# A recurrent cell's candidate product with its weights stationary, r and z in one PSUM bank, and z taken late as 1 - z

## The chip, the cores and the metric

The kernel runs on one NeuronCore of a Trainium2 chip. The metric is device time in microseconds (us): the median of several runs of the program. A profile of one execution comes with it; its times count from the first instruction.

The engines are named as in the profile: PE is TensorE's matmul, PEld its weight load, DVE is VectorE, ACT is ScalarE, POOL is GpSimd, SP issues most DMAs. Each engine runs its own instructions in the order in which the program lists them, and waits where an operand is not yet there.

## The reference

Four layers stand one behind the other, each added to its input x of shape 8 x 512 x 256 (batch, time, features), all in float32: a mixture of experts, a gated Haar transform, an adapter with low-rank weights made from a condition, and a gated recurrent unit over the 512 time steps. Only the last one is touched:

```
def step(H, xs):                       # 512 times, H is 8 x 256
    xz, xr, xh = xs                    # X @ Wx.T + bx, for all steps
    Z = sigmoid(xz + H @ Whz.T + bhz)
    R = sigmoid(xr + H @ Whr.T + bhr)
    H_tilda = tanh(xh + R * H @ Whh.T + bhh)   # (R * H) @ Whh.T
    H_new = Z * H + (1.0 - Z) * H_tilda
    Y = H_new @ Whq.T + bhq
    return (H_new, Y)
```

Step s needs the state of step s - 1, so the 512 steps cannot overlap each other.

## The kernel before

The time axis is cut into 16 windows of 32 steps. The first three layers of a window are a few hundred pieces of work ("jobs") on PE, ACT, DVE, POOL and SP. A prologue computes window 0 and the condition's weights. Then one Python loop writes out the 512 recurrent steps (L1362 to L1493), and between the instructions of a step it puts jobs of the later windows and of the output product (`Whq`, L1252). The order on each engine is written by this loop: `jobs.fill(engine, due, most)` (L159) takes up to so many jobs whose inputs a plan believes to be there at time `due`, and the plan assumes that a step lasts `STEP` = 2.43 us. A PE job is as a rule one `quads` call (L482): four products of 128 x 32 weights with 256 columns, one for each 32 rows of the output. PE jobs have two places in a step: `first_slot` behind the products of r and z, `second_slot` behind the candidate's product.

One float32 product is two weight loads and two matmuls in the profile. So "x16" in a row below is eight products in the program.

The state is kept feature-major, 128 partitions x 2 feature chunks x 8 batch columns, in four rotating tiles `s_h[u]`. A step does this:

- `recur` for r (L1400): `across` (L1194) takes the state as the stationary operand (32 columns, of which 8 are this step's) and 64 columns of `wh` as the moving one, for both chunks k and four output quarters. The result is batch-major, in the bank of `rh[:, n, 0]` (tile `grh`).
- Sigmoid on ACT in two halves (L1403), a copy of the last state into `hist` (L1405), two DVE transposes back to feature-major (`rT`, L1407), two DVE products with the state (`s_rh`, L1409).
- `recur` for z (L1412) into another bank (`gz`), sigmoid (L1417), transpose, z * h (L1422) and 1 - z (L1423) on DVE.
- The PE jobs of the first slot (L1446) and, in part, the input's projections of a coming group of four steps (`project`, L1228: 128 columns for r and the candidate together, 64 for z).
- `recur` for the candidate (L1451), with `s_rh` as the stationary operand, into `rh[:, n, 1]`; tanh in two halves (L1455); the second slot (L1458); two transposes (L1465).
- Two `tensor_tensor_scan` of 16 elements (L1469), one per chunk. For every batch column it runs over two elements (d0, d1): (0, candidate), then (1 - z, z * h), with state = d0 * state + d1. This gives the new state.

`biases` (L1208) writes the bias rows into the PSUM banks by ACT copies ahead of the projections, for 16 steps at a time. `implied` (L249) tells the framework that a dependency is covered by another one; all other waits are set by the framework.

Of the kernel before, what the change touches and what calls it, by code (L numbers as in the profile page):

```python
# [16 lines left out]
P = 128  # L17
B, T, C = 8, 512, 256
KC = C // P
# [37 lines left out]
STEP = 2.43  # L57
# [80 lines left out]
class Jobs:  # L138
# [56 lines left out]
    def drain(self, now=0.0):  # L195

        while any(q for d in (self.queues, self.urgent, self.last) for q in d.values()):
            for eng, most in (("SP", 9), ("PE", 2), ("ACT", 2), ("DVE", 3), ("POOL", 3)):
                self.fill(eng, now, most)
            now += 1.0  # L200
# [3 lines left out]
def cond_resid_kernel(  # L204
# [81 lines left out]
    ps_g = pool_of("ps_g", 2, PSUM)  # L286
    ps_z = pool_of("ps_z", 1, PSUM)
    gz = ps_z.tile([P, 2, NG, FQ], F32, name="gz")

    def new_gates(c):  # L290
        rh = ps_g.tile([P, NG, 2, FQ], F32, name=f"grh_{c}", tag="grh")
        return rh, gz[:, c % 2]

    both = [new_gates(c) for c in range(2)]
    zeros = const.tile([P, NT], F32, name="zeros")
    nc.vector.memset(zeros, 0.0)
    rh0, rh1 = [g[0].rearrange("p n g f -> p (n g f)") for g in both]
# [14 lines left out]
    claim(gz.rearrange("p c n f -> p (c n f)"))  # L312
    claim(rh0)
# [92 lines left out]
    r_c = Ring(None, "c", None, 1, rh1)  # L406
# [16 lines left out]
    for g, n in enumerate((0, 2, 1)):  # L423
        got_wx = load(wx[:, :, g, :], rows_of(sq_b[:, ts(n, C)]), 0.25)
# [36 lines left out]

    own = const.tile([P, B], F32, name="own")
# [680 lines left out]

    xts = [Lazy(r_xt) for w in range(NW)]
# [11 lines left out]
    jobs.run([l0_ends[0], *got_low_in, *got_small, got_wx, got_wh])  # L1156
# [11 lines left out]
    with (  # L1168
# [7 lines left out]
        G_R, G_ZH, G_HH, G_Q = 0, 1, 2, 3  # L1176
        RH, G_Z = slice(0, 2), 2
        RH_STORED = slice(0, 3, 2)

        s_h, s_rh, d0s = [], [], []
        for u in range(GS):
            s = gw.tile([P, KC, GS, B, 2], F32, name=f"s_h{u}")
            nc.vector.memset(s, 0.0)
            s_h.append(s)
            s = gw.tile([P, KC, GS, B], F32, name=f"s_rh{u}")
            nc.vector.memset(s, 0.0)
            s_rh.append(s)
            s = gw.tile([P, KC, B, 2], F32, name=f"d0_{u}")  # L1190
            nc.vector.memset(s, 0.0)
            d0s.append(s)
# [15 lines left out]
        def biases(gates):  # L1208

            rh, z = gates  # L1210

            def bias(out, row):
                groups = out.shape[1]
                shape = [P, groups, *row.shape[1:]]
                if row.shape[1] == FQ:
                    row = row.rearrange("p (o f) -> p o f", o=1)
                else:
                    row = row.rearrange("p (o g) f -> p o g f", o=1)
                return nc.scalar.copy(out, row.broadcast_to(shape))

            half = NG // 2
            return [
                lambda: bias(rh[:, :half], brow[:, RH_STORED]),
                lambda: bias(rh[:, half:], brow[:, RH_STORED]),
                lambda: bias(z, brow[:, 1]),
            ]

        def project(g, gates):  # L1228

            rh, z = gates  # L1230
            n, w = g % NG, g * GS // WS
            of = ends[w][g * GS % WS * len(ends[w]) // WS]
            assert all(j.done is not None for j in of), g
            x = xts[w].get()
            t0 = g * GS % WS
            parts = []
            for k in range(KC):
                xk = x[:, k, t0 : t0 + GS, :]
                parts.append(lambda k=k, xk=xk: across(rh[:, n], xk, wx[:, k, RH]))
                parts.append(lambda k=k, xk=xk: across(z[:, n], xk, wx[:, k, G_Z]))  # L1240
            return parts

        def recur(out, g, s):
            made = []
            for k in range(KC):
                made += across(out, s(k), wh[:, k, g])
            return made

        def state(u):
            return lambda k: s_h[u][:, k, :, :, 1]  # L1250

        def output_jobs(c, hist, copied, a=0, n=TC):  # L1252

            held = c >= HELD
            queue = jobs.last if held else jobs.urgent
            t0 = c * TC
# [25 lines left out]
            for m in range(KC):  # L1282
# [3 lines left out]
                for k in range(KC):  # L1286
# [10 lines left out]
                        0.45,  # L1297
                        queue,
# [12 lines left out]
        gates = both[0]  # L1311
        for part in biases(gates):
            part()
# [3 lines left out]
        for g in range(2):  # L1317
            for part in project(g, gates):
                part()
        nc.vector.tensor_copy(s_h[0][:, :, 0, :, 1], h0)  # L1320
# [13 lines left out]
        def first_slot(s, at):  # L1334

            if any(j.done is None for j in ends[1][0]) or jobs.ending() and jobs.left("PE"):
                return 1
            if jobs.left("PE"):
                return 1 if behind(s) and jobs.ready("PE", at + 1.0) > 1 else 0
            return 1 if len(jobs.last["PE"]) > T - s else 0  # L1340

        def second_slot(s, at):
# [11 lines left out]
        z_bias = None  # L1354
# [4 lines left out]
            g: [gw.tile([P, FQ], F32, name=f"{g}_{i}") for i in range(2)] for g in "rzc"  # L1359
        }  # L1360
        upcoming, parts, bias_parts = gates, [], []
        for c in range(NTC):  # L1362
            hist = hists[c]
            gates = upcoming
            for t in range(TC):
                s = c * TC + t
                n, u = t // GS, t % GS
                v = (u + 1) % GS
                rh, z = gates
                now = base + s * STEP  # L1370
# [4 lines left out]
                def gate(pre, func, name, parts=1):  # L1375
# [3 lines left out]
                        nc.scalar.activation(x, y, func)  # L1379
# [11 lines left out]
                def transposed(dst, src, name):  # L1391
# [5 lines left out]
                    used[(name, s % 2)].append(ins)  # L1397

                h = s_h[u][:, :, u, :, 1]
                made = recur(rh[:, n, 0], G_R, state(u))  # L1400
                for mm in made:
                    implied(mm, *acted, *biased)
                r, act_r = gate(rh[:, n, 0], AF.Sigmoid, "r", KC)  # L1403
                if copying is not None:
                    copying(now + 1.0)  # L1405
                rT = gs.tile([P, KC, GS, B], F32, name=f"rT_{s}", tag="rT")
                for k in range(KC):  # L1407
                    transposed(rT[:, k : k + 1], chunk(r, k), "r")
                for k in range(KC):  # L1409
                    prod = tt(s_rh[u][:, k, u, :], rT[:, k, u, :], h[:, k], ALU.mult)  # L1410
                    implied(prod, *readers.get(("rh", u), ()))
                made_z = recur(z[:, n], G_ZH, state(u))  # L1412
                for mm in made_z:
                    implied(mm, *acted, *(b for b in biased if b is not z_bias))
                z_bias = None
                readers[("h", u)] = made + made_z
                zg, act_z = gate(z[:, n], AF.Sigmoid, "z")  # L1417
                zT = gs.tile([P, KC, GS, B], F32, name=f"zT_{s}", tag="zT")
                transposed(zT, zg, "z")
                d1 = gs.tile([P, KC, GS, B, 2], F32, name=f"d1_{s}", tag="d1")  # L1420
                d0 = d0s[u]
                tt(d1[:, :, u, :, 1], zT[:, :, u, :], h, ALU.mult)  # L1422
                nc.vector.tensor_scalar(  # L1423
                    d0[:, :, :, 1], zT[:, :, u, :], -1.0, 1.0, ALU.mult, ALU.add
                )
                jobs.fill("DVE", now + 1.66, 1, of=[jobs.small["DVE"]])
                jobs.fill("SP", now, 1)


# [3 lines left out]
                if c == 0 and t == 4:  # L1433
                    claim(rh1)
                if c + 1 < NTC and t == 6:
                    upcoming = new_gates(c + 1) if c else both[1]
                    bias_parts = biases(upcoming)
                if 2 * GS <= ahead < T:
                    if ahead % GS == 0:
                        assert not parts  # L1440
                        of = upcoming if ahead // TC > c else gates
                        parts = project(ahead // GS, of)
                    part = parts.pop(0)
                    if ahead % WS == WS - 1:
                        projected[ahead // WS].done = now + 1.0
                jobs.fill("PE", now + 0.5, first_slot(s, now + 0.5))  # L1446
                if part is not None and ahead % 2 == 0:
                    part()
                    part = None
                jobs.fill("ACT", now + 1.15, 1)  # L1450
                made = recur(rh[:, n, 1], G_HH, lambda k, q=s_rh[u]: q[:, k])  # L1451
                for mm in made:
                    implied(mm, *acted, *biased, *act_r)
                readers[("rh", u)] = made
                cand, act_c = gate(rh[:, n, 1], AF.Tanh, "c", KC)  # L1455
                if part is not None:
                    part()
                jobs.fill("PE", now + 1.44, second_slot(s, now + 1.44))  # L1458
                if bias_parts and t >= 7:
                    biased.append(bias_parts.pop(0)())  # L1460
                    if not bias_parts:
                        z_bias = biased[-1]
                else:
                    jobs.fill("ACT", now + 1.95, 1)
                for k in range(KC):  # L1465
# [96 lines left out]
```

## Time and profile before

| what | value |
|---|---|
| median of 3 runs | 1321.74 us (1320.26 to 1321.94) |
| the profiled execution, first to last instruction | 1316.5 us |
| granted PE clock, mean | 0.998 |
| PE busy | 1178.3 us, 89% |
| DVE busy | 916.8 us, 70% |
| ACT busy | 505.7 us, 38% |
| DMA | 46.46 MB, mean 35 GB/s |
| copies of the state into `hist` (one per step) | 512, first start 71.7 us, last 1310.9 us |

The 511 intervals between these copies are (1310.9 - 71.7) / 511 = 2.425 us each. 512 steps of 2.42 us are 1239 us of the span; the remaining 77.5 us are the prologue, some stalls in the first steps, and the end. The busy shares are sums over overlapping work: a PE that is 89% busy has 138 us without a matmul in flight.

### The profile page before, as it was taken

How to read it: one execution, taken by the hardware profiler on the slowest of the kernel's cores; microseconds unless marked ns; L12 is line 12 of the kernel's file. 1: busy time of each engine (PE TensorE's matmuls, PEld its weight loads, DVE VectorE, ACT ScalarE, POOL GpSimd, SP SyncE). 2: the span in 40 equal slices, each digit the busy share in tenths (PEclk: the TensorE clock that was granted, in tenths of full speed). 3: DMA queues.
4: the chain of work that ended last, by engine and by line, in shares of the span. 5: the costliest groups of instructions: out<-in, count | busy, mean ns of one | idle time of the engine just before them, and what ended most of it. 6: DMA issues, size and time to landing. Idle time of an engine off the chain costs nothing.

```text
span 1316.5 us, 88999 instructions
## 1 busy us (share of the span) xinstructions
PE 1178.3 (89%) x39240; PEld 688.4 (52%) x39240; DVE 916.8 (70%) x6271; ACT 505.7 (38%) x3407; POOL 150.6 (11%) x235
## 2 busy tenths in 40 slices
PE   8999999899999999998888988888888888878886
PEld 5666555555555555555554555545554545545443
DVE  5367777777776767676776767677676767667775
ACT  2134343444344444334343433443434344433332
POOL 3311110101011110101011010101101011110000
PEclk9999999999999999999999999999999999999999
DMA  9910001200010010100000010000001000000111
GB/s 318 352 53 16 5 4 38 52 5 29 13 36 20 12 29 5 52 4 28 12 15 26 4 36 4 22 19 12 28 4 29 12 4 4 4 4 4 36 30 26
DMA packets 41859, 46.46 MB, mean 35 GB/s; under 512 B 27488, under 2 KB 31104, under 8 KB 40320
## 3 DMA queue, kind: packets, MB, share of 16 engines
q1 hardware_dynamic: 38576, 38.31, 9.5%
q8 instruction: 306, 5.01, 1.6%
q0 software_dynamic: 1184, 2.31, 0.5%
q14 instruction: 81, 0.66, 0.2%
q10 hardware_dynamic: 1712, 0.16, 0.1%
HBM read 36.45 MB, written 4.33 MB: 31 GB/s over the span
## 4 chain that ended last, share of the span: by engine, by line
PE 66%; DVE 19%; ACT 9%; issue 4%; DMA 2%; SPq 0%; ACTq 0%
PE grh L1197 35%; PE hp L485 11%; DVE d L1393 7%; DVE rT L1393 6%; PE acc L485 6%; PE gz L1197 5%; ACT c L1379 5%; PE low L485 4%; ACT r L1379 4%; PE misc L485 3%; DVE s_h L1469 3%; DVE s_rh L1410 2%; DMA bc<-comb_d 1%; DMA sw_sb<-in_sw_dram 0%; PE misc L1104 0%
## 5 line engine op out<-in xcount | busy, mean ns | idle before, releaser
L1393 DVE STREAM_TRANSPOSE rT<-r 128x32 f32<-128x32 f32 x1024 | 156.1, 191 | 219.5 <-ACT r L1379 215.8
L1379 ACT ACTIVATE r<-grh 128x32 f32<-128x32 f32 x1024 | 146.3, 195 | 421.0 <-PE grh L1197 418.2
L1197 PE MATMUL grh<-wh,s_h 128*32 128x64 f32 x8192 | 221.8, 225 | 90.1 <-DVE s_h L1469 89.1
L1197 PEld LDWEIGHTS grh<-wh,s_h 128*32 128x32 f32 x8192 | 140.4, 109 | 309.6 <-DVE s_h L1469 308.4
L1379 ACT ACTIVATE c<-grh 128x32 f32<-128x32 f32 x1024 | 146.2, 195 | 313.6 <-PE grh L1197 313.1
L1197 PE MATMUL grh<-wh,s_rh 128*32 128x64 f32 x8192 | 221.6, 225 | 34.3 <-DVE s_rh L1410 10.0
L1197 PEld LDWEIGHTS grh<-wh,s_rh 128*32 128x32 f32 x8192 | 139.2, 108 | 191.8 <-DVE s_rh L1410 188.1
L1393 DVE STREAM_TRANSPOSE d<-c 128x32 f32<-128x32 f32 x1024 | 156.5, 192 | 115.2 <-ACT c L1379 108.9
L1197 PE MATMUL gz<-wh,s_h 128*32 128x64 f32 x8192 | 209.9, 219 | 0.4 <-issue 0.3
L1197 PEld LDWEIGHTS gz<-wh,s_h 128*32 128x32 f32 x8192 | 153.5, 110 | 0.9 <-issue 0.8
L485 PE MATMUL acc<-g,rw_sb 128*32 128x256 f32 x2048 | 153.5, 379 | 0.0
L485 PE MATMUL hp<-x,sw_sb 128*32 128x256 f32 x2016 | 150.8, 384 | 2.6 <-ACT sig L583 2.2
L634 POOL TENSOR_TENSOR g<-gl,bc 128x256 f32<-128x256 f32 x128 | 93.6, 733 | 511.9 <-DVE s_h L1469 358.8
L485 PE MATMUL hp<-x,rw_sb 128*32 128x256 f32 x2016 | 151.4, 380 | 0.7 <-ACT sig L617 0.6
L1469 DVE TENSOR_TENSOR_SCAN s_h<-d,d 128x16 f32<-128x16 f32 x1024 | 145.4, 184 | 0.0
L1410 DVE TENSOR_TENSOR s_rh<-rT,s_h 128x8 f32<-128x8 f32 x1024 | 133.5, 168 | 0.0
L1393 DVE STREAM_TRANSPOSE zT<-z 128x64 f32<-128x64 f32 x512 | 121.9, 238 | 0.4 <-ACT z L1379 0.3
L1379 ACT ACTIVATE z<-gz 128x64 f32<-128x64 f32 x512 | 121.4, 237 | 0.8 <-PE gz L1197 0.4
L1483 ACT COPY hist<-s_h 128x16 f32<-128x16 f32 x512 | 106.3, 208 | 0.5 <-DVE s_h L1469 0.5
L1197 PE MATMUL grh<-wx,xt 128*32 128x128 f32 x2048 | 104.8, 274 | 1.3 <-ACT r L1379 1.1
L1422 DVE TENSOR_TENSOR d<-zT,s_h 128x16 f32<-128x16 f32 x512 | 90.7, 177 | 17.5
L1423 DVE TENSOR_SCALAR d<-zT 128x16 f32<-128x16 f32 x512 | 86.8, 169 | 0.0
(154 smaller groups left out, 1208.7 us busy)
## 6 DMA issues: line engine op xcount, KB each, us to landing
bc<-comb_d SPq DMA_DIRECT2D x56, 256.0 KB, 3.2
w<-in_w_dram SPq DMA_DIRECT2D x5, 1024.0 KB, 13.5
out_dram<-x SPq DMA_DIRECT2D x14, 256.0 KB, 3.2
x<-in_w_dram SPq DMA_DIRECT2D x3, 1024.0 KB, 15.6
x<-in_xT_dram SPq DMA_DIRECT2D x2, 1536.0 KB
bc<-comb_d POOLq DMA_DIRECT2D x8, 256.0 KB, 9.0
sw_sb<-in_sw_dram SPq DMA_DIRECT2D x3, 512.0 KB, 8.0
wsq_a<-in_sq_a_dram SPq DMA_DIRECT2D x1, 1280.0 KB
```

The lines of the kernel that those rows point to most:

```text
L485: nc.tensor.matmul(out[ts(j, 32)], lhs[:, ts(j, 32)], rhs, start=start, stop=False, skip_group_check=True,)
L634: lambda gl=gl, g=g, e=e: nc.gpsimd.tensor_tensor(g.get(), gl.get(), bcs[e // 2].get()[:, e % 2], ALU.mult),
L1197: nc.tensor.matmul(out[ts(j, 32)], lhs, rhs[:, ..., ts(j, FQ)], start=start, stop=False, skip_group_check=True,)
L1379: nc.scalar.activation(x, y, func)
L1393: ins = nc.vector.transpose(dst.rearrange("p i u b -> p i (u b)"), src.rearrange("p (i r) -> p i r", r=32),)
L1410: prod = tt(s_rh[u][:, k, u, :], rT[:, k, u, :], h[:, k], ALU.mult)
L1422: tt(d1[:, :, u, :, 1], zT[:, :, u, :], h, ALU.mult)
L1423: nc.vector.tensor_scalar(d0[:, :, :, 1], zT[:, :, u, :], -1.0, 1.0, ALU.mult, ALU.add)
L1469: new = nc.vector.tensor_tensor_scan(s_h[v][:, k, v].rearrange("p b w -> p (b w)"), d0[:, k].rearrange("p b w -> p (b w)"), d1[:, k, u].re ...
L1483: nc.scalar.copy(hist[:, :, t, :], s_h[v][:, :, v, :, 1])
```

## The change

The candidate's product is turned round: the weights `wh[:, k, G_HH]` become the stationary operand (128 x 32 at a time) and r * h, 8 columns, the moving one. The result comes out feature-major, in two banks `cand[m]` (one for each chunk of 128 features), and tanh writes it straight into the scan's operand `d1`. The two transposes of the candidate are gone, and 16 products of 8 columns take the place of 8 products of 64.

r and z lie side by side in one PSUM bank `rz`. The products with chunk 0 of the state are made for both gates at once (128 columns); chunk 1 follows for r alone (64 columns), and, behind the first slot, for z alone. z's sigmoid takes the scale -1, which gives 1 - z; its transpose goes straight into `d0`. The scan now runs over three elements: (0, c), (1, -h), (1 - z, h). So z * h and 1 - z are no longer made; instead two DVE products write -h and h.

The projections are split: r and z together, 128 columns, two `across` per four steps; the candidate's for 16 steps at once (`project_c`, four parts of 128 columns). The jobs of the output product get a place of their own between z's products and the candidate's. The plan's step is 2.6 us for the first 28 steps and 2.24 us behind.

```diff
-STEP = 2.43
+STEP, FIRST_STEP, FIRST = 2.24, 2.6, 28
...
+    rz = ps_g.tile([P, NG, 2, FQ], F32, name="grz")
+    cand = [ps_g.tile([P, NG, TC, B], F32, name=f"gc{m}") for m in range(KC)]
...
+        def turned(out, w, m, rhs):
+            return [
+                nc.tensor.matmul(
+                    out[ts(j, 32)],
+                    w[:, FQ * j + 32 * m : FQ * j + 32 * m + 32],
+                    rhs,
...
+                for j in range(NQ)
+            ]
...
-                made = recur(rh[:, n, 0], G_R, state(u))
+                made = across(rz[:, n], of(0), wh[:, 0, RZ])
+                made += across(rz[:, n, 0], of(1), wh[:, 1, G_R])
...
-                made_z = recur(z[:, n], G_ZH, state(u))
...
-                zg, act_z = gate(z[:, n], AF.Sigmoid, "z")
...
-                transposed(zT, zg, "z")
...
-                tt(d1[:, :, u, :, 1], zT[:, :, u, :], h, ALU.mult)
-                nc.vector.tensor_scalar(
-                    d0[:, :, :, 1], zT[:, :, u, :], -1.0, 1.0, ALU.mult, ALU.add
-                )
+                for k in range(KC):
+                    both_h = tt(
+                        d1[:, k, :, 1:3],
+                        h[:, k].rearrange("p (b o) -> p b o", o=1).broadcast_to([P, B, 2]),
+                        signs,
+                        ALU.mult,
+                    )
...
                 jobs.fill("PE", now + 0.5, first_slot(s, now + 0.5))
...
+                made_z = across(rz[:, n, 1], of(1), wh[:, 1, G_Z])
...
+                        for mm in c_parts.pop(0)():
...
+                    jobs.fill("PE", now + 1.05, 1, of=[jobs.small["PE"]])
+                jobs.fill("ACT", now + 0.95, 1)
+                zg, act_z = gate(rz[:, n, 1], "z", 1, -1.0)
+                if s % GS == 2 and 2 * GS <= s + 6 < T:
+                    biased = biased[-8:] + [rz_bias(s // GS + 2)]
...
-                made = recur(rh[:, n, 1], G_HH, lambda k, q=s_rh[u]: q[:, k])
+                for m in range(KC):
+                    for k in range(KC):
+                        made += turned(cand[m][:, c % NG, t], wh[:, k, G_HH], m, rh[:, k])
...
-                cand, act_c = gate(rh[:, n, 1], AF.Tanh, "c", KC)
+                act_c = [
+                    nc.scalar.activation(d1[:, m, :, 0], cand[m][:, c % NG, t], AF.Tanh)
+                    for m in range(KC)
+                ]
...
                 if part is not None:
-                    part()
-                jobs.fill("PE", now + 1.44, second_slot(s, now + 1.44))
+                    for mm in part():
+                        implied(mm, *acted, *biased, *act_r)
+                jobs.fill("PE", now + 1.6, second_slot(s, now + 1.6))
...
-                for k in range(KC):
-                    transposed(d1[:, k : k + 1, :, :, 0], chunk(cand, k), "c")
+                turn_z = transposed(d0[:, :, :, :, 2], zg, "z")
...
                     new = nc.vector.tensor_tensor_scan(
                         s_h[v][:, k, v].rearrange("p b w -> p (b w)"),
-                        d0[:, k].rearrange("p b w -> p (b w)"),
-                        d1[:, k, u].rearrange("p b w -> p (b w)"),
+                        d0[:, k, u].rearrange("p b w -> p (b w)"),
+                        d1[:, k].rearrange("p b w -> p (b w)"),
```

## The prediction, made before the changed kernel ran

> **What bounds the kernel now.** I read the page first, for the chain of work that ended last:
>
> ```profile
> span 1316.5 us, 88999 instructions
> ...
> PE 66%; DVE 19%; ACT 9%; issue 4%; DMA 2%; SPq 0%; ACTq 0%
> ```
>
> PE, DVE and ACT share the chain and no DMA does, so what sets the end is a loop through three engines. The timeline in the middle shows one step (start us, length us):
>
> ```profile
> 703.23 0.43 PE L1197 MATMUL grh<-wh,s_h 128*32 128x64 f32 x16 [0.24 <-DVE s_h L1469]
> ...
> 703.48 0.41 PE L1197 MATMUL gz<-wh,s_h 128*32 128x64 f32 x16
> ...
> 703.70 0.61 PE L485 MATMUL acc<-g,rw_sb 128*32 128x256 f32 x8
> 703.73 0.29 ACT L1379 ACTIVATE r<-grh 128x32 f32<-128x32 f32 x2 [0.93 <-PE grh L1197]
> ...
> 703.96 0.30 DVE L1393 STREAM_TRANSPOSE rT<-r 128x32 f32<-128x32 f32 x2 [0.37 <-ACT r L1379]
> 703.99 0.24 ACT L1379 ACTIVATE z<-gz 128x64 f32<-128x64 f32 x1
> 704.07 0.20 PEld L1197 LDWEIGHTS grh<-wx,xt 128*32 128x32 f32 x8 [0.23 <-ACT r L1379]
> 704.13 0.40 PE L1197 MATMUL grh<-wx,xt 128*32 128x128 f32 x8
> 704.21 0.26 DVE L1410 TENSOR_TENSOR s_rh<-rT,s_h 128x8 f32<-128x8 f32 x2
> ...
> 704.43 0.43 PE L1197 MATMUL grh<-wh,s_rh 128*32 128x64 f32 x16
> ...
> 704.92 0.29 ACT L1379 ACTIVATE c<-grh 128x32 f32<-128x32 f32 x2 [0.69 <-PE grh L1197]
> 705.15 0.31 DVE L1393 STREAM_TRANSPOSE d<-c 128x32 f32<-128x32 f32 x2 [0.24 <-ACT c L1379]
> 705.40 0.19 DVE L1469 TENSOR_TENSOR_SCAN s_h<-d,d 128x16 f32<-128x16 f32 x1
> ```
>
> In the chain of waits the next r product starts at 705.65, so the step lasts 2.42. From start to start: r products 0.50, sigmoid 0.23, transposes 0.25, r*h 0.22 (sum 1.20), candidate's products 0.49, tanh 0.23, transposes 0.25, scan 0.25 (sum 1.22). Everything else, PE's jobs included, fits around this loop.
>
> Two rows elsewhere price narrow products: one in the prologue with 8 columns, one near the end with 32.
>
> ```profile
> 26.13 1.06 PE L1034 MATMUL grh<-lnc,wsq_a 128*128 128x8 f32 x8
> ...
> 1306.51 0.30 PE L485 MATMUL hp<-hist,wh 128*32 128x32 f32 x8
> ```
>
> **PE's prices.** Rows come in fours, one for each 32 output rows, side by side. The gz row starts 0.25 behind the r row and the acc row 0.22 behind gz: 0.055 for a four of 64 columns. The 128-column row lasts 0.40 with 0.27 for one: its two fours start 0.11 apart, with 0.02 of stagger. A 256-column job (eight rows) is 0.43 in the chain of waits.
>
> **The change, part by part.**
>
> *r products.* Two fours of 128 columns and two of 64 replace four of 64. Last start 0.11 + 0.11 + 0.055 + 0.02 = 0.30, against 0.43 - 0.22 = 0.21 before. Cost +0.08; the candidate's product starts at 1.28.
>
> *Candidate's product.* 32 rows of 8 columns replace 16 of 64: eight fours, four for each half. No row has this form. From below: the 8-column row lasts 1.06 with 0.26 for one, 0.114 between neighbours, each loading 128 columns; a quarter of the columns, four side by side, is 0.028 a four. From above: 0.055, as if the columns did not matter. Between them the 32-column row: 0.30 with 0.24 for one, less 0.02 of stagger, 0.04 a four; its moving operand is strided, which makes 128-column rows last 0.40 instead of 0.27. I take 0.028, from the row with the same 8 columns. The second half of r*h comes 0.09 behind the first (0.26 less 0.17), so the fours of the first half start at 0, 0.06, 0.10, 0.13 and the last row at 0.15, not 0.21. Mean lengths 379, 274 and 219 ns at 256, 128 and 64 columns fall by 0.83 ns a column, so 172 ns at 8: another 0.05. tanh starts 0.38 behind the product's start, 0.11 earlier than now.
>
> The Trainium skill speaks against this: "TensorEngine Tiling (Array Packing)", section "Performance Considerations" under "Instruction Overhead", gives every product some 60 cycles, so that one column is as slow as 60. By it a four would cost 60/64 of 0.055, and the total would be an estimated 1310 us. The 8-column row contradicts neither: it loads four times as many columns.
>
> *tanh.* 8 columns instead of 32: 195 ns at 32 and 237 at 64 give 1.3 ns a column, so 0.03 less; nothing if the length is fixed. I take 0.20 to the scan.
>
> *Candidate's transposes.* Off the loop: -0.25.
>
> *Scan.* 24 elements instead of 16. DVE's products are 168 ns at 8 and 177 at 16, 1.1 ns an element: +0.01, or +0.02 at two passes. I take 0.265.
>
> The loop is then 1.28 + 0.38 + 0.20 + 0.265 = 2.12. The candidate's second half runs 0.11 behind the first, and is wanted 0.22 later, behind the first 128-column fours: hidden.
>
> *z late, in r's bank.* z's second products now wait for ACT to leave the bank, as the projection does at 704.07, 0.05 behind ACT's end. r's sigmoid ends at 0.58 + 0.29 = 0.87, z's products start at 0.92 and their last row at 1.02, its sigmoid starts 0.28 later at 1.30 and ends at 1.54, the transpose ends at 1.80. The scan wants it at 1.28 + 0.38 + 0.20 = 1.86: 0.06 to spare. On DVE the removed 0.24 + 0.18 + 0.17 pays for two products (about 0.28) and the transpose that moved in front of the scan. On ACT, z's bias copy (128 x 128, 282 ns for that size) stands ahead of tanh in one step of four; ACT starts an instruction some 0.11 before the one ahead ends (the state's copy starts at 703.90 and lasts 0.21, z starts at 703.99), so tanh could start at 1.30 + 0.13 + 0.17 = 1.60, and starts at 1.66 anyway. POOL's and SP's queues gain only memsets ahead of the loop; I count nothing for them, since the prologue's PE work covers them. PE's zeroing of the second candidate bank (two jobs' worth, 0.86) moves from step 4 into the prologue, which leaves the sum as it is.
>
> *PE's jobs.* The same work (588 us in slots against 590) must fit a shorter step. The candidate's products stream until 1.28 + 0.27 = 1.55; a projection part (0.215) waits for z's sigmoid, 1.54 + 0.05 = 1.59. In the program's listed order the work behind the candidate's products is:
>
> - at most one job, 242 steps: 1.98, under the loop, so 2.12
> - part and one job, 143 steps: 1.59 + 0.645 = 2.235
> - two jobs, 18 steps: 1.55 + 0.86 = 2.41
> - part and two jobs, 109 steps: 1.59 + 1.075 = 2.665
>
> In 52 steps more than 0.25 of work stands between z's and the candidate's products, mostly one output job: 1.03 + 0.43 = 1.46 instead of 1.28, +0.18 each.
>
> **Sum.** 242 x 2.12 + 143 x 2.235 + 18 x 2.41 + 109 x 2.665 + 52 x 0.18 = 513.0 + 319.6 + 43.4 + 290.5 + 9.4 = 1175.9, 2.30 a step. Before, 512 x 2.42 = 1239.0 of 1316.5: 77.5 lie around the steps and stay. Span 1253.4. The median of the runs lies 1321.74 - 1316.5 = 5.2 above the profiled span, so 1258.6: I say 1258.
>
> **Rivals.**
>
> *PE's jobs don't bind.* The pieces behind the candidate start earlier than I think, and all steps run at the loop's 2.12: 1085 + 77.5 + 5.2 = 1168, or partly, up to 1210. For it: my wait of the projection on z is inferred from one row. Against: two jobs alone are 0.86 of a half that has 0.85 left in all. 0.10.
>
> *z becomes the wait.* With 0.06 to spare, a sigmoid job of 0.39 ahead of z's on ACT, or a late first-slot job, delays the scan and every projection part. 0.15 late in every step: 0.09 x 242 + 0.15 x 252 = 60 us, 1318; in half of the steps 1288. For it: z's products wait for r's sigmoid, where they now run without a wait. Against: ACT is 38% busy. 0.15.
>
> *Narrow products cost as wide ones.* Four rows of 8 columns at 0.055: fours until 0.47, tanh at 0.44, loop 2.18; behind the candidate's end at 1.75 the four classes take 2.18, 2.40, 2.61, 2.83: 527.6 + 343.2 + 47.0 + 308.5 + 9.4 = 1235.7, total 1318. That is 2.2 us for each ns of a four; from 0.057 on the kernel is slower, and at 0.07 it would be 1350. For it: the 64-column fours could be set by their loads, which are as wide here. Against: the 32-column row, 0.04. 0.11, of which 0.09 slower.
>
> **Chances and range.** The forecast has 0.64. What a measurement of this kernel can tell from no change is about 0.2%, 2.6 us. Faster 0.64 + 0.10 + 0.15 = 0.89, within 0.02, slower 0.09. The range 1210 to 1310: the low end has half of the PE-bound excess gone ((1258 - 1168) / 2 is 45), the high end a four at 0.051 or z late in most steps. Left out are most of the first rival and the third, about 0.2.
>
> **What would show it.** Right: 32 rows of the candidate's product start within 0.30 of each other; tanh 0.38 behind their start; steps in two kinds, near 2.12 and near 2.67, the long ones with 16 rows of 256 columns and a projection ahead of r's products; no transpose of the candidate; r's sigmoid 0.58 behind its products. Wrong: a wait of the scan on z's transpose; tanh 0.45 or more behind the candidate's start; steps of one length. The prediction fails by a lot if the narrow rows don't run four side by side.

## The result, and the profile after

The changed kernel takes 1344.6 us (median of 4 runs, 1342.95 to 1345.76), the kernel before 1321.84 on the same chip. The ratio is 1.0175, 95% interval 1.016 to 1.0189: slower, where the forecast said 1258 and faster. The profiled execution has a span of 1344.0.

The page of the changed kernel, the span and the chain that ended last by engine:

```profile
span 1344.0 us, 94890 instructions
...
PE 85%; ACT 5%; issue 4%; DVE 3%; DMA 2%; POOL 0%; ACTq 0%; DVEq 0%; POOLq 0%
```

PE was 66% of the chain and DVE 19%. The loop through three engines has become a chain of PE's products. The timeline in the same place shows a long step, 702.78 to 705.52, and a short one behind it (start us, length us):

```profile
702.78 0.55 PE L1200 MATMUL grz<-wh,s_h 128*32 128x128 f32 x16
...
703.40 0.29 ACT L1401 ACTIVATE r<-grz 128x32 f32<-128x32 f32 x2 [0.59 <-PE grz L1200]
...
703.74 0.33 PE L1200 MATMUL grz<-wh,s_h 128*32 128x64 f32 x8
...
704.10 0.47 PE L1242 MATMUL gc<-rh,wh 128*32 128x8 f32 x32
704.14 0.22 ACT L1401 ACTIVATE z<-grz 128x64 f32<-128x64 f32 x1 [0.36 <-PE grz L1200]
704.39 0.27 DVE L1415 STREAM_TRANSPOSE d<-z 128x64 f32<-128x64 f32 x1
704.41 0.43 PE L1200 MATMUL grz<-wx,xt 128*32 128x128 f32 x8
704.57 0.28 ACT L1484 ACTIVATE d<-gc 128x8 f32<-128x8 f32 x2 [0.20 <-PE gc L1242]
704.66 0.61 PE L490 MATMUL hp<-x,rw_sb 128*32 128x256 f32 x8
704.78 0.31 DVE L1501 TENSOR_TENSOR_SCAN s_h<-d,d 128x24 f32<-128x24 f32 x2
...
705.09 0.61 PE L490 MATMUL acc<-g,sw_sb 128*32 128x256 f32 x8
...
705.52 0.51 PE L1200 MATMUL grz<-wh,s_h 128*32 128x128 f32 x16
...
706.84 0.22 ACT L1401 ACTIVATE z<-grz 128x64 f32<-128x64 f32 x1
707.10 0.27 ACT L1213 COPY grz<-brow 128x128 f32<-128x128 f32 x1
...
707.30 0.25 ACT L1484 ACTIVATE d<-gc 128x8 f32<-128x8 f32 x2
707.51 0.31 DVE L1501 TENSOR_TENSOR_SCAN s_h<-d,d 128x24 f32<-128x24 f32 x2
707.77 0.55 PE L1200 MATMUL grz<-wh,s_h 128*32 128x128 f32 x16
```

In the first step the scan starts at 704.78, but PE still has a projection part and two 256-column jobs to issue, and r's next products start at 705.52 instead of 0.26 behind the scan. Two more waits can be seen. z's transpose ends at 704.66, the scan follows 0.12 behind it, and tanh had started 0.21 ahead of the scan, so the two come in a dead heat. In the second step the bias copy at 707.10 starts only when z's sigmoid is over (706.84 + 0.22), though both are ACT's own. In the trace all of the loop's copies carry a wait on ACT's own semaphore, which the framework sets, and they start 0.03 behind the sigmoid's end. Tanh comes behind the copy: 0.50 behind the candidate's products (706.80) instead of 0.40.

Measured over 511 steps from the starts of these rows in the trace (my own sums; means in us):

```
piece of the loop               before  forecast  after   e9
scan to r's products             0.251    0.427   0.413   0.311
r's products to r's sigmoid      0.501    0.58    0.642   0.729
r's sigmoid to r*h               0.475    0.475   0.484   0.485
r*h to candidate's products      0.225    0.243   0.260   0.241
candidate's products to tanh     0.499    0.38    0.435   0.414
tanh to scan                     0.477    0.20    0.245   0.219
sum                              2.429    2.305   2.481   2.399
```

The forecast's first row holds its mean of 0.162 for PE's jobs, the fourth its 52 late candidates (9.4 us / 512 = 0.018). The path from the candidate to the scan did shrink, by 0.296 a step; PE's jobs took back 0.162, r's longer products 0.141, the rest 0.044: 0.052 more in all.

### The profile page after: what moved, and what is told of

It reads as the page before. It is cut to its first block, busy times and chain, and to the rows that moved or that the text cites. A ratio compares the mean times of both kernels' runs of the same rounds, so it can differ in the third digit from the quotient of the medians.

```text
span 1344.0 us, 94890 instructions
## 1 busy us (share of the span) xinstructions
PE 1278.4 (95%) x42312; PEld 781.8 (58%) x42312; DVE 831.9 (62%) x5244; ACT 587.8 (44%) x3503; POOL 150.9 (11%) x241
## 4 chain that ended last, share of the span: by engine, by line
PE 85%; ACT 5%; issue 4%; DVE 3%; DMA 2%; POOL 0%; ACTq 0%; DVEq 0%; POOLq 0%
PE grz L1200 32%; PE hp L490 18%; PE gc L1242 15%; PE acc L490 11%; PE low L490 6%; PE misc L490 3%; ACT z L1401 1%; DVE s_h L1501 1%; ACT grz L1213 1%; ACT r L1401 1%; DMA h<-in_condT_dram 1%; DVE rT L1415 1%; ACT d L1484 1%; DVE rh L1437 1%; DMA comb_d<-cT 1%
## 5 line engine op out<-in xcount | busy, mean ns | idle before, releaser
L1200 PEld LDWEIGHTS grz<-wh,s_h 128*32 128x32 f32 x12288 | 332.5, 125 | 397.3 <-ACT r L1401 217.2
L1200 PE MATMUL grz<-wh,s_h 128*32 128x64 f32 (+1 forms) x12288 | 458.0, 246 | 26.2 <-ACT r L1401 11.5
L1401 ACT ACTIVATE r<-grz 128x32 f32<-128x32 f32 x1024 | 146.2, 195 | 427.4 <-PE grz L1200 427.0
L1242 PE MATMUL gc<-rh,wh 128*32 128x8 f32 x16384 | 242.5, 181 | 18.8 <-issue 5.9
L1242 PEld LDWEIGHTS gc<-rh,wh 128*32 128x32 f32 x16384 | 202.9, 111 | 83.1 <-DVE rh L1437 58.0
L1501 DVE TENSOR_TENSOR_SCAN s_h<-d,d 128x24 f32<-128x24 f32 x1024 | 168.8, 202 | 74.9 <-ACT d L1484 22.1
L1484 ACT ACTIVATE d<-gc 128x8 f32<-128x8 f32 x1024 | 164.7, 181 | 74.8 <-PE gc L1242 35.9
L1415 DVE STREAM_TRANSPOSE d<-z 128x64 f32<-128x64 f32 x512 | 138.0, 269 | 47.3 <-ACT z L1401 15.4
L1437 DVE TENSOR_TENSOR rh<-rT,s_h 128x8 f32<-128x8 f32 x1024 | 133.8, 170 | 1.4 <-PE grz L1200 0.7
L1440 DVE TENSOR_TENSOR d<-s_h,signs 128x16 f32<-128x16 f32 x1024 | 130.5, 169 | 0.0
```

Source lines behind the costliest of these rows:

```text
L1200: nc.tensor.matmul(out[ts(j, 32)], lhs, rhs[:, ..., ts(j, FQ)], start=start, stop=False, skip_group_check=True,)
L1242: nc.tensor.matmul(out[ts(j, 32)], w[:, FQ * j + 32 * m : FQ * j + 32 * m + 32], rhs, start=False, stop=False, skip_group_check=True,)
L1401: nc.scalar.activation(x, y, AF.Sigmoid, scale=scale)
L1415: ins = nc.vector.transpose(dst.rearrange("p i u b -> p i (u b)"), src.rearrange("p (i r) -> p i r", r=32),)
L1437: prod = tt(rh[:, k], rT[:, k, u, :], h[:, k], ALU.mult)
L1440: both_h = tt(d1[:, k, :, 1:3], h[:, k].rearrange("p (b o) -> p b o", o=1).broadcast_to([P, B, 2]), signs, ALU.mult,)
```

## The experiments

Five theories are named in the expectations. A: the waits of the shared bank and of the late z cost the gain. B: PE's jobs stacked behind the candidate's products do. C: the narrow products are no gain. D, formed after the fourth run: PE's code (its instructions, which a DMA queue brings in while it runs) can't come in faster. E, its rival: PE's work itself is too much. A "part" is one of the two pieces of the projection for four steps. The ratio is to the kernel before on the same chip; the changed kernel has 1.0175.

```
run                           median us  ratio   95% interval
e1_z_with_r                     1349.5   1.0239  1.0219 to 1.0258
e2_two_jobs_other_steps         1320.3   1.0009  0.9999 to 1.0019
e3_no_rz_bias                   1336.8   1.0134  1.0118 to 1.0149
e4_own_banks                    1459.9   1.1071  1.1044 to 1.1098
e5_own_banks_wide               1410.0   1.0674  1.0652 to 1.0695
e6_own_banks_wide_two_jobs      1391.8   1.0542  1.0526 to 1.0558
e7_shared_bank_wide_two_jobs    1433.0   1.0861  1.0823 to 1.0898
e8_before_z_in_halves           1434.0   1.0861  1.0845 to 1.0878
e9_z_with_r_jobs_first          1304.2   0.9878  0.9862 to 0.9895
e10_bias_for_two_groups         1312.4   0.9942  0.9927 to 0.9957
e11_late_z_jobs_first           1322.6   1.0013  1.0000 to 1.0025
```

**e1: z no longer late.**

```
-                made += across(rz[:, n, 0], of(1), wh[:, 1, G_R])
+                made += across(rz[:, n], of(1), wh[:, 1, RZ])
...
-                made_z = across(rz[:, n, 1], of(1), wh[:, 1, G_Z])
```

> From the changed kernel: z's second products are made together with r's, as one row of 128 columns, so nothing of z is made behind r's sigmoid; the bank stays shared. Theory A (late z and the shared bank are what costs: in the changed kernel the scan waits for z's transpose in about half of the steps, and r's products to r's sigmoid take 0.64 us instead of 0.50): tanh to scan falls from 0.245 to 0.20, but r's products to sigmoid grow from 0.64 to about 0.75 because two fours of 64 columns become fours of 128; 512 x (0.11 - 0.045 - 0.02 for the bias copy that no longer stands behind a late z) = about +20 us, 1355 to 1370. If the late z alone were what ate the gain, the scan would no longer wait and the time falls to 1320 or below. Theory B (PE's jobs behind the candidate's products set the long steps): the long steps stay as they are, and only the steps of one job or less move, by about +0.06: 1355 to 1365.

r's products to sigmoid grew by 0.10 as expected, the scan waits for z's transpose in none of the 511 steps (after: in 283 tanh to scan is over 0.235), and candidate to tanh and the candidate's start gained 0.02 and 0.03. Sum: 0.6% slower than the changed kernel, just under the ranges of both theories, which had the direction right. So making z late costs no more than it saves; it is not what ate the gain. The mean of the 132 steps longer than 2.6 is 2.86, as before the edit.

**e2: the jobs in other steps.**

```
-            two = behind(s, 8) or (s + 5) % 2 == 0 and behind(s)
+            two = behind(s, 8) or (s + 5) % 2 == 1 and behind(s)
```

> From the changed kernel: two 256-column jobs are issued behind the candidate's products in the steps that have no part of the projection (they now fall on those that have one). The work is the same. Theory B (the jobs stacked in the second half set the end of 109 steps at 2.79 to 2.85 us): behind the candidate's products, part and two jobs go from 109 steps to 15, part and one job from 142 to 223, two jobs from 18 to 108; at the measured 2.83, 2.40 and 2.47 (estimate between the others) for them and 2.31 for the rest the mean step falls by about 0.05 to 0.06, 25 to 30 us: 1314 to 1322. Theory A (the waits of the bank and of z) or theory C (the turned products are dear): the place of the jobs is the same within 5 us, 1340 to 1350.

1.6% less with the same work (1.0009 / 1.0175), inside theory B's range. The kernel stands level with the one before. In the trace the gain is where B puts it: scan to next products falls from 0.413 to 0.365.

**e3: no bias copies in the loop.**

```
-                if s % GS == 2 and 2 * GS <= s + 6 < T:
-                    biased = biased[-8:] + [rz_bias(s // GS + 2)]
```

> From the changed kernel: the loop's copies of r's and z's bias into the shared bank are left out (so r and z carry no right bias after the first groups; the output is not the reference's). Theory A: in every fourth step the copy stands between z's sigmoid and tanh, and waits for z's because both touch the bank: products of the candidate to tanh 0.50 us there against 0.41; one step later r's sigmoid starts 0.68 behind r's products against 0.58 to 0.62, because it waits for ACT's copy and PE. (0.095 + 0.08) / 4 = 0.044 a step, about 20 us less: 1320 to 1328. Theory B: these steps are partly set by PE anyway and only the quiet ones gain, under 8 us: 1336 to 1344.

0.4% less, about 5 us, at B's figure and far from A's. The two places do what A said: one step behind a copy r's sigmoid comes at 0.63 instead of 0.69, and in the step with the copy tanh at 0.44 to 0.47 instead of 0.48 to 0.49. But in the other steps tanh now comes 0.02 to 0.06 later: in the trace a semaphore instruction stands ahead of it in 383 steps (after: 37), for a second wait, on ACT's own semaphore beside PE's, and there tanh starts 0.303 behind the sixteenth row of the products instead of 0.243. It seems that the copy had carried this second wait. The changed kernel's r sigmoid shows the same price: in the 126 steps behind a copy it has two waits and starts 0.346 behind its sixteenth row, elsewhere 0.286. So the 20 us of this expectation can't be had by this edit, and it doesn't price the bank alone.

**e4: the turned candidate alone.**

```
-    rz = ps_g.tile([P, NG, 2, FQ], F32, name="grz")
-    cand = [ps_g.tile([P, NG, TC, B], F32, name=f"gc{m}") for m in range(KC)]
+    gr = ps_g.tile([P, 2, NG, FQ], F32, name="gr")
+    gz = ps_g.tile([P, 2, NG, FQ], F32, name="gz")
+    cand = ps_g.tile([P, KC, 2, TC, B], F32, name="gc")
...
-                made = across(rz[:, n], of(0), wh[:, 0, RZ])
-                made += across(rz[:, n, 0], of(1), wh[:, 1, G_R])
+                made = across(gr[:, n], of(0), wh[:, 0, G_R])
+                made += across(gr[:, n], of(1), wh[:, 1, G_R])
...
+                made_z = across(gz[:, n], of(0), wh[:, 0, G_Z])
+                made_z += across(gz[:, n], of(1), wh[:, 1, G_Z])
```

> From the changed kernel: of the change only the turned candidate and the scan of three remain. r and z have a bank each again, z's products (64 columns) follow r's at once without a wait for r's sigmoid; the candidate's two halves share a bank, so tanh of the first half waits for both halves' products; the bias copies are one for two groups. Theory A (bank sharing and late z cost, the turn itself gains): r's products to sigmoid 0.50, transposes and r*h 0.47, candidate's start at 1.22 to 1.24, tanh 0.47 to 0.53 behind it (all 32 rows instead of 16), scan 0.21 later, next products 0.265 later: loop 2.17 to 2.25; with the long steps of PE's jobs on top (0.10 to 0.15 in the mean) 1275 to 1310, below both kernels. Theory B (PE's jobs bind whatever the loop is): 1310 to 1335. Theory C (32 narrow rows are no gain against 16 of 64 columns and two transposes): 1335 or above.

Only C's open range, 1335 or above, takes in 1460, and C's cause isn't there: the medians of the loop's pieces add up to what A expected, 0.262 + 0.514 + 0.230 + 0.246 + 0.224 + 0.543 + 0.214 = 2.233. But the mean step is 2.704. The waits of PE (total us, times, longest) show on what:

```profile
PE gc L1250 <- issue: 42.0, 74, 2.3
PE gz L1202 <- issue: 22.4, 42, 1.5
...
PE gr L1202 <- issue: 17.2, 39, 2.1
PE hp L492 <- issue: 14.2, 26, 1.7
```

"issue" means that PE waited for nothing that the profile shows. It is 107 us here, and stands in front of any kind of product. One such wait in the chain, in the middle of a job of eight rows:

```profile
704.85 0.42 PE acc L492 x4
705.27 0.38 issue
705.66 0.27 PE acc L492
```

I numbered PE's rows (a weight load and its matmul) by their starts. In the loop 89 of these stalls are longer than 0.45 us, and all 88 distances between neighbours are a multiple of 128 rows to within 5. The queue table of the page shows what has this period:

```profile
q8 instruction: 378, 6.19, 1.8%
```

378 packets of 16 KB, for 48456 rows with a weight load each: 256 instructions, 128 rows, a packet. So PE stands still where its code comes to the end of a block. The times of the packets in the trace say so too. In e4's loop they start 3.74 us apart in the mean and never under 3.2, and 128 rows in 3.74 us are 34.2 a us. Of the 140 stalls over 0.3 us nine in ten end 1.2 to 1.5 us behind the end of a packet; of times picked at random, nine in ten lie 0.2 to 3.6 behind one. The mean time of 8 rows, at the rows where a block begins and elsewhere (us):

```
kernel   rows a step   rows a us   at the start of a block   elsewhere
before       74.5        30.7         none stands out      0.230 to 0.288
after        80.5        32.5         0.281 and 0.260          0.242
e4           92.4        34.2         0.572 and 0.292          0.206
e8           90.4        34.2              0.509               0.216
e9           72.5        30.3         none stands out      0.252 to 0.284
```

Some 369 blocks with 0.45 each are 167 us; without them e4 would take an estimated 1293, which is in A's range. This became theory D.

**e8: code alone, in the kernel before.** This run settles D, since the change has no part in it.

```
-                made_z = recur(z[:, n], G_ZH, state(u))
+                made_z = []
+                for k in range(KC):
+                    for i in range(2):
+                        made_z += [
+                            nc.tensor.matmul(
+                                z[ts(j, 32), n, ts(i, 32)],
+                                state(u)(k),
+                                wh[:, k, G_ZH, FQ * j + 32 * i : FQ * j + 32 * i + 32],
...
```

> The kernel before the change with one edit: z's products of 64 columns are made as two of 32, same work and same result, 16 rows more in a step (90.5 instead of 74.5). z's rows are off the chain that sets the step of 2.42. Theory D: at 34.2 to 35.5 rows a us 90.5 rows need 2.55 to 2.65 a step: 1385 to 1440, with stalls at every 128th row. Theory E: a four of 32 columns at 0.04 instead of half of 0.055 makes z's products 0.10 to 0.15 longer, in a half step in which PE has some room: 1320 to 1360, and no stall at a fixed place.

8.6% slower, 113 us, inside D's range. Rows come in at 34.2 a us, the rate of e4, and the stalls are there, again in front of any product:

```profile
PE gz L1416 <- issue: 27.0, 49, 1.8
...
PE grh L1197 <- issue: 20.4, 46, 1.6
```

0.293 at each of 362 blocks are 106 us, nearly all of the loss; the chain's other pieces keep their medians. Here too the packets start 3.75 us apart. In the kernel before, the waits in front of PE that the profile calls "issue" are 2.4 us, in the changed one 12.8.

**e5, e6, e7: fewer and wider rows.** The candidate's matrix is loaded 64 columns wide, 16 rows a step instead of 32. e5 is e4 with this; e6 has e2's slot rule too; e7 is the changed kernel with both.

```
-                    out[ts(j, 32)],
-                    w[:, FQ * j + 32 * m : FQ * j + 32 * m + 32],
+                    out[ts(j, 64)],
+                    w[:, m, ts(j, 64)],
...
-                for j in range(NQ)
+                for j in range(P // 64)
```

> The kernel of e4 with one edit: the candidate's stationary matrix is loaded 64 columns wide instead of 32, so that a product makes two blocks of 32 output rows and the candidate takes 16 rows of 8 columns in a step instead of 32 (a copy of the matrix in that order is made once ahead of the loop). Theory D (PE's code): in e4 PE stands still at every 128th row, at the same place in the order of its rows, and from there to the next such place take 3.74 us in the mean, at least about 3.4; 92 rows a step are 34.2 rows a us, which is the most that its code comes in. With 76 rows a step the stalls go: chain as in e4's undisturbed steps 0.26 + 0.51 + 0.23 + 0.25 + 0.22 + 0.54 to 0.60 + 0.21 = 2.23 to 2.29, and 0.08 to 0.15 for long steps: 1270 to 1320. Theory E (PE's work itself, more and narrower rows than before, is too much for the step): the same columns are loaded and streamed, and only half of the candidate's rows go away, so at most 0.2 a step of the 2.70: 1360 or above.

> The kernel of e5 with the slot rule of e2 (two 256-column jobs behind the candidate in the steps without a part of the projection). Theory B and D together (jobs set the long steps, code loads no longer interfere): 15 to 25 us below e5, 1250 to 1300. If code is still the limit at 76 rows a step, the place of the jobs is the same within 5 us.

> The changed kernel with the slot rule of e2 and the candidate's matrix 64 columns wide as in e5: bank sharing and late z stay. Against e2 (80.5 rows a step) only the rows change, to 64.5. Theory D: e2 loses about 0.07 us at every 128th row, 320 times, some 20 us, and those go: 1295 to 1310. If the wider rows lengthen the first half of the candidate by more than 0.05, 0.05 x 512 = 25 us are given back and it stays at 1320. Theory E or bank waits alone: 1315 to 1335.

e5's stalls are gone: 1.3 us of "issue" on PE in all, 29.0 rows a us. But it gains 50 us, not at least 140: candidate to tanh grew from a median of 0.543 to 0.685. In the groups (busy us, mean ns of one) of the changed kernel and of e5, half as many rows of the same 8 columns take longer:

```profile
L1242 PE MATMUL gc<-rh,wh 128*32 128x8 f32 x16384 | 242.5, 181 | 18.8 <-issue 5.9 <-DVE rh L1437 0.9
```

```profile
L1259 PE MATMUL gc<-rh,turn_h 128*64 128x8 f32 x8192 | 325.5, 205 | 47.1 <-DVE rh L1460 20.4
```

So D's time for e5 was wrong, by the price of the wide rows and by long steps (2.61 in the mean where the medians add up to 2.42), though the stalls went as it said. The time lies in E's open range, 1360 or above; but E had put e4's loss down to PE's work alone, and 107 us of "issue" went with the rows. e6 stands 18 us below e5 (expected 15 to 25), B once more; its range of 1250 to 1300 fell with e5's. e7 is a plain miss: it loses to e2 by 113 us, although it has no stalls (24 rows a us); there the candidate's last row starts 0.436 behind the first instead of 0.291, which pushes PE's jobs on, and scan to next products grows from 0.365 to 0.547.

**e9: z with r, and the jobs ahead of the candidate.** e1 plus:

```
-                return 1 if behind(s) and jobs.ready("PE", at + 1.0) > 1 else 0
+                return 2 if behind(s) and jobs.ready("PE", at + 1.0) > 2 else 1
...
-            two = behind(s, 8) or (s + 5) % 2 == 0 and behind(s)
+            two = behind(s, 8)
...
-            return 2 if two and jobs.ready("PE", at + 1.0) > 2 else 1
+            return 1
```

> The kernel of e1 (z's second products together with r's) with other slot rules: where the kernel is behind, two 256-column jobs are issued between r's and the candidate's products, and behind the candidate's products one. Theory B: in e1 a step with at most 0.86 of jobs ahead of the candidate and 0.43 behind it lasts 2.31, with a part and one job behind it 2.42, with a part and two jobs 2.84 (108 steps). By the listed order this kernel has some 260 steps of the first kind, 230 of the second, 22 with two jobs or more behind (2.7), and 42 with 1.08 or more ahead of the candidate (+0.1 to +0.3): mean 2.39 against 2.48, 44 us less than e1's 1349: 1295 to 1315, below both kernels by about 1%. Theory D alone (code) would leave e1's time, since at 72.5 rows a step its rows are only 29 to 30.5 a us: 1340 to 1350. If the late candidate takes back what the end of the step gains: 1325 to 1340.

1304.2, in the middle of B's range, and faster than both kernels: 0.9878 of the one before, 0.971 of the changed one (0.9878 / 1.0175). Its timeline shows a step with two jobs (16 rows of 256 columns) ahead of the candidate and one behind it:

```profile
702.54 0.62 PE L1200 MATMUL grz<-wh,s_h 128*32 128x128 f32 x16
...
702.98 1.05 PE L490 MATMUL hp<-x,sw_sb 128*32 128x256 f32 x16
703.23 0.29 ACT L1401 ACTIVATE r<-grz 128x32 f32<-128x32 f32 x2 [0.90 <-PE grz L1200]
...
703.50 0.24 ACT L1401 ACTIVATE z<-grz 128x64 f32<-128x64 f32 x1
...
703.93 0.47 PE L1242 MATMUL gc<-rh,wh 128*32 128x8 f32 x32
704.05 0.27 DVE L1415 STREAM_TRANSPOSE d<-z 128x64 f32<-128x64 f32 x1
704.23 0.62 PE L490 MATMUL hp<-x,sw_sb 128*32 128x256 f32 x8
704.34 0.34 ACT L1481 ACTIVATE d<-gc 128x8 f32<-128x8 f32 x2 [0.30 <-PE gc L1242]
704.55 0.36 DVE L1498 TENSOR_TENSOR_SCAN s_h<-d,d 128x24 f32<-128x24 f32 x2 [0.23 <-ACT d L1481]
...
704.81 0.66 PE L1200 MATMUL grz<-wh,s_h 128*32 128x128 f32 x16
```

z's sigmoid follows r's at once, both jobs fit between r's products and the candidate's, and r's next products start 0.26 behind the scan: 2.27. Only 36 steps are longer than 2.6 (after: 151). The kernel before has next to nothing to gain from its jobs' places: scan to r's products is 0.251 in the mean and 0.246 in the shortest fifth of its steps, r*h to the candidate's products 0.225 and 0.222.

**e10: e9 with fewer bias copies.**

```
-            return nc.scalar.copy(rz[:, g % NG], brow[:, RZ])
+            a = g % NG
+            return nc.scalar.copy(
+                rz[:, a : a + 2],
+                brow[:, RZ].rearrange("p (o n) f -> p o n f", o=1).broadcast_to([P, 2, 2, FQ]),
+            )
```

> The kernel of e9 with r's and z's bias copied for two groups in every eighth step, instead of one in every fourth. In e1 the r sigmoid one step behind the copy starts 0.79 behind r's products against 0.69 elsewhere; half of these steps go: 64 x 0.10 = 6 us below e9. If the larger copy (256 columns) delays tanh, the gain is lost: same as e9 within 3 us.

A miss, 8 us slower. In one step of eight r's sigmoid comes 0.06 earlier, as expected, but in four of eight tanh comes 0.03 to 0.06 later (0.47 instead of 0.41 to 0.44), as in e3.

**e11: e9's slots, but z late.** The changed kernel with the slot rules of e9.

> The changed kernel (z's second products late) with the slot rules of e9. Behind the candidate's products the listed work is nearly that of e9 (242 steps with one job, 227 with a part and one, 22 with more), but 113 steps now have two jobs between r's products and z's late ones. Theory A (late z): there z's products start at 0.30 + 0.86 = 1.16 behind r's instead of 0.92, z's transpose ends 0.93 later at about 2.1 and the scan starts at 2.2 instead of 1.9: +0.3 in 113 steps, against some 15 us less than e2 from the end of the step: 1325 to 1345, at least 20 above e9. Theory B alone: the end of the step decides, so the same as e9 or, with r's products 0.1 shorter, less: 1260 to 1305.

18 us above e9 and 1.6% below the changed kernel, just under A's range and well above B's. Against e9 it starts the sigmoid 0.093 earlier, and gives that back: tanh to scan 0.048, candidate's start 0.038, candidate to tanh 0.031, and the code ceiling (33.1 rows a us; 0.303 at the start of a block against 0.24). How its 18 us divide between the late z and the code isn't settled by this run.

## Why the prediction was wrong

By its own steps, a step of the loop being 2.481 where 2.305 was forecast: 512 x 0.176 = 90 us, and the span is 1344.0 where 1253.4 was forecast.

- **PE's jobs** were sized right: 0.413 from scan to r's products against 0.427. The two kinds of step are there, with 2.32 in the mean for steps up to 2.6 and 2.86 for the 151 above. In part this is luck, since both ends moved: in the 109 steps with a part and two jobs the part starts 1.74 behind r's products (forecast 1.59), and the scan 2.08 (forecast 1.86). e2 and e9 show that this term can be moved (22 us, and 45 from e1 to e9), and that it was the largest single cost of the change.
- **The loop of 2.12** is the step that failed. 0.58, 0.38 and 0.20 are the least values of r's products to sigmoid, candidate to tanh and tanh to scan, or below them: in the trace one fifth of the steps have 0.580, 0.401 and 0.209 or less. The means are 0.642, 0.435 and 0.245: +32, +28 and +23 us. And 0.58 is not even what an undisturbed loop has: in the 118 steps in which r's products start within 0.275 of the scan and the step before had no copy, their second four starts 0.149 behind the first and the sigmoid 0.620 behind them, 0.12 more than before the change and not 0.08; in the 265 in which they start later it is 0.109 and 0.580 (medians). The forecast had its 0.11 from a projection's row of the kernel before, which started while a job's matmuls still ran (704.13, the job until 703.70 + 0.61). I added up undisturbed pieces and let only PE's jobs disturb them.
- **"0.06 to spare" for z** was wrong. The forecast let the scan start where z's transpose ends; the trace has some 0.12 between them. So the scan waits for z in 283 of 511 steps, 0.05 each in the median and 0.06 in the mean, some 18 of the 23 us. That rival had the mechanism, but at 0.15 a step far too dear; e1 shows that its cure costs at least as much.
- **The other rivals.** That PE's jobs don't bind fell with the first row of the table. The one that was to make the kernel slower, dear narrow rows, didn't come true; it became slower by the sum of smaller waits instead.
- **"tanh could start 1.60, starts 1.66 anyway"** was wrong. The bias copy, in z's bank, waits for z's sigmoid to be over, where I had ACT start 0.11 ahead of that. In those steps tanh comes 0.07 later, 9 us in all, and r's sigmoid, with its second wait, 0.06 later one step on, 7 us. e3 shows both places, though not the sum.
- **The candidate's products**: 32 rows start within 0.291 of each other in the median (forecast: within 0.30) and the sixteenth 0.164 behind the first (0.15). Narrow rows do run four side by side, and theory C fell with e4's 2.233. Per four that is 0.291 / 7 = 0.042, where I took 0.028 and the third rival needed 0.055. The Trainium skill's rule of 60 cycles, which "TensorEngine Tiling (Array Packing)", "Performance Considerations", gives under "Instruction Overhead", would make it 0.052 by the forecast's own estimate; the measured 0.042 is under that, so that the columns still count.
- **What had no line in the forecast** is PE's code. 80.5 rows in 2.30 us are 35.0 a us, more than the 34.2 that two kernels reached: 80.5 / 34.2 = 2.354 a step, so 512 x 2.354 + 77.5 + 5.2 = 1288 was about the least that this change could give with its rows, whatever its waits. In the changed kernel the blocks cost an estimated 322 x 0.057 = 18 us, spread over the pieces above; its "issue" waits are 12.8 us. The Trainium skill speaks of it in "Runtime: NRT & Kernel Launch", section "Instruction fetch mechanics": code is streamed in blocks of 16 KB, and crossing a block is mostly hidden. Block and packet agree (378 packets, 6.19 MB); "mostly hidden" holds at 30 rows a us, and not at 34.

Of the 32 us of r's products some 9 are the 0.04 of the second four (118 steps and 115 behind a copy), 7 the second wait behind the copies, and 12 lie in 36 other steps with more than 0.65. What holds those up stays open.

## What to carry to other kernels

A shorter loop is worth only what the engine that fills its gaps can still place: list the work for each half-step against the new length, and move it before counting the gain. Sum a loop from means of its pieces, with every wait that shares a bank or a second semaphore, not from its undisturbed pieces. Count the products a us that the new step asks of PE, and compare with the highest rate that any run has shown.

## What the runs showed of the hardware

- PE's code was the limit at 34.2 rows a us (a row is a weight load and a matmul) in e4 and in e8, two different kernels, with packets of code 3.74 and 3.75 us apart. PE then stands still, for up to 2.3 us, at places a multiple of 128 rows apart, in the profile as "issue".
- Where r's products started within 0.275 of the scan, their second four of 128 columns came 0.149 behind the first; where they started later, 0.109.
- Sixteen rows of 8 columns with 64 columns loaded took longer (325.5 us busy, tanh 0.685 behind their start) than 32 rows with 32 loaded, four side by side (242.5 to 269.2 us, 0.543).
- An activation with a second semaphore to wait for started 0.06 later (tanh 0.303 instead of 0.243, r's sigmoid 0.346 instead of 0.286 behind the row it waits for). So taking away an instruction can make its neighbour later, as in e3 and e10.
